# A sixteen-sequence RWKV, tree, attention and expert block: the products u times gate and the splitting of the maxima on GpSimd, and other figures in the planner

## The chip, the cores and the metric

The kernel runs on one core of a Trainium2 chip. The core has a matrix engine (TensorE, "PE" in the profile, its weight loads "PEld"), a vector engine (VectorE, "DVE"), a scalar engine with function tables (ScalarE, "ACT"), a general-purpose vector engine (GpSimd, "POOL"), and a queue that issues transfers ("SP"). Each works through its own queue of instructions in order, and waits on semaphores where it needs another's result. The metric is the device time of one execution in microseconds (us), the median of several executions.

## What is computed

The input x has 16 sequences of 512 tokens with 128 features. Four blocks follow each other, each with a residual and a layer norm:

```
x = layernorm(x + rwkv(x))       # two layer norms, time mix with a scan over the tokens, channel mix
x = layernorm(x + tree(x))       # 255 sigmoid routers, 256 leaf probabilities, leaf values
x = layernorm(x + attention(x))  # RMS norm, rotary positions, 16 heads of 8, causal softmax
x = layernorm(x + experts(x))    # 16 experts, the two of greatest gate kept, and a shared part
```

Two parts bear on the change. In the experts block, with u the normed input,

```
s = softmax(u @ centroids.T + bias)
g = s where s is one of the two greatest of its token, else 0
out = u + sum over e of g[e] * (u @ Wr[e].T + br[e]) + shared(u)
```

and in attention the softmax over the keys subtracts the greatest score of each query and head.

## The kernel before

Features (or the chunks of 128 of the 512 hidden ones) lie on the partitions, and the 512 tokens of one sequence run along a tile, so that most instructions work on 128x512 numbers in f32. A sequence passes through these pieces, each a Python generator:

- `front` (line 458): the first norms, RWKV, tree and the rotated queries and keys. RWKV runs in four chunks (`rwkv`, line 503), two of them at a time. Each has products k, r and v on TensorE, two scans over the tokens on VectorE (sk and skv), the sum sk on GpSimd, two more steps of skv and the reciprocal of sk on VectorE, and the product rw on GpSimd. TensorE then multiplies rw by the output weights into p.
- `operands` (697) loads queries and keys, split in three bf16 parts, for one of four groups of four heads, into one of three sets of buffers.
- `greatest` (718) makes all scores of a group on TensorE (sc), takes their maxima on VectorE (nmx, 128x16 numbers), splits these in three bf16 parts (nm3), transposes the parts on TensorE (pmx) and puts them as extra rows into the queries.
- `weighted`, `sums` and `ends` make the scores again, transposed (st), their exponentials on ScalarE (ew), the weighted sums on TensorE (o) and the attention's output up to u, the experts' input.
- `gating` (863) makes the gates. They go to DRAM and come back as gb, spread over the partitions, two experts to a transfer, in two buffers.
- `by_gate` (937) makes the experts' operands us = u * gate, one 128x512 product for each of 16 experts, in three buffers. `experts` (951) multiplies each by its weights and adds it into the bank acc; a buffer comes free with that product.

The order of the work isn't the order of the program text. A planner (`Plan`, line 55) holds all pieces in a queue by time, runs the one that is due first, and with each instruction moves that engine's clock on by a cost: `tensor_us` (154), `vector_us` (163), `pool_us` (172) and a cost for ScalarE. The instructions are issued in the order in which the planner comes to them, and `issue_after` (137) keeps that order on each engine. A bare `yield` hands over once the piece's last instruction is done by the planner's clock; slots stand for buffers and PSUM banks. The planner runs when the kernel is built. Its clock decides the order alone; on the chip only the order and the semaphores are left.

A front starts when the one before it has come to its event "mixed" (591, after its channel mix), but not before its due time by the planner's clock:

```python
yield event("mixed", b - 1)
yield max(0.0, PERIOD * b - LEAD - plan.now)
```

So several sequences are under way at once: RWKV of one, attention of the one before, and experts of the one before that.

Of the kernel before, what the change touches and what calls it, by code (L numbers as in the profile page):

```python
# [12 lines left out]
ALU = mybir.AluOpType  # L13
# [3 lines left out]
B, T, D = 16, 512, 128  # L17
# [23 lines left out]
HAND_OVER = 0.2  # L41
BANKS = 8
SCORES = 4
PERIOD = 125.0
LEAD = 60.0
RWKV_PACE = 10.0
EXPERT_PACE = 3.0
MAX_PACE = 0.0
# [98 lines left out]
def columns(ap):  # L147
    n = 1
    for d in ap.shape[1:]:
        n *= d  # L150
    return n


def tensor_us(op, out, w, x, *_):
    n = columns(out)
    if out.shape[0] == 32:
        return 0.05 + 0.0009 * n
    if x.dtype == BF16:
        return 0.02 + 0.00044 * n
    return 0.01 + 0.0009 * n if op == "transpose" else max(0.25, 0.00177 * n)  # L160


def vector_us(op, out, *args):
# [6 lines left out]


def pool_us(op, out, *_):
    return 0.5 + 0.0019 * columns(out)


@with_exitstack
def rwkv_tree_attn_moe(ctx: ExitStack, tc: tile.TileContext, a: dict, out: bass.AP):
# [18 lines left out]
    def scalar_us(op, out, x, f=None, *_):  # L196
        us, wanted = 0.2 + 0.00078 * columns(out), {AF.Ln: "ln", AF.Tanh: "tanh"}.get(f, table[0])
        if wanted != table[0]:
            table[0] = wanted
            us += 1.3  # L200
        return us

    mm, tr, act, copy = (Engine(plan, "PE", nc.tensor, tensor_us).matmul, Engine(plan, "PE", nc.tensor, tensor_us).transpose,
                         Engine(plan, "A", nc.scalar, scalar_us).activation, Engine(plan, "A", nc.scalar, scalar_us).copy)
    V, G = Engine(plan, "V", nc.vector, vector_us), Engine(plan, "G", nc.gpsimd, pool_us)
    banks, scores, chunks, sets = Slots(plan, BANKS), Slots(plan, SCORES), Slots(plan, 2), Slots(plan, OPERANDS)
    e_slots, us_slots, gb_slots = Slots(plan, 2), Slots(plan, 3), Slots(plan, 2)
    held, happened = {}, {}

    def event(*key):  # L210
        return happened.setdefault(key, Event(plan))
# [7 lines left out]
    def load_x(b):  # L219
        x0 = p2.tile([128, T], F32, tag="x0", name="x0")  # L220
        nc.sync.dma_start(out=x0, in_=a["xT"][:, b * T:(b + 1) * T])
        return x0
# [190 lines left out]
    def bank(name, shape=(128, 512), dtype=F32):  # L413
        i = yield banks
        p = ps.tile(list(shape), dtype, tag=f"b{i}", name=name)
        held[id(p)] = p, i
        return p

    def give(p):
        banks.put(held.pop(id(p))[1])  # L420
# [37 lines left out]
    def front(b, keep):  # L458

        if b:  # L460
            yield event("mixed", b - 1)
            yield max(0.0, PERIOD * b - LEAD - plan.now)
        x0 = load_x(b) if b else first_x
# [254 lines left out]
    def greatest():  # L718

        for b in range(B):  # L720
            for g in range(NG):
                yield event("ops", b, g)
                _, qo, ko = kept[b]["ops", g]
                nmx = p2.tile([128, NT, HG], F32, tag="nmx", name="nmx")
                for t in range(NT):
                    w = (t + 1) * 128
                    per = min(HG, 512 // w)
                    for h in range(0, HG, per):
                        slot = yield scores
                        sc = yield from bank("sc", (128, per, w))  # L730
                        for i in range(per):
                            mm(sc[:, i, :], qo[:, h + i, t * 128:w], ko[:, h + i, 0:w], start=(i == 0), stop=False)
                        mm(sc[:, :, t * 128:w], identb, masks[:, 0:per, :], start=False, stop=True)
                        yield
                        V.tensor_reduce(nmx[:, t, h:h + per], sc, AX.X, ALU.max, negate=True)
                        give(sc)
                        scores.put(slot)
                        if MAX_PACE:
                            yield MAX_PACE
                nm3 = p2.tile([128, NT, PARTS, HG], BF16, tag="nm3", name="nm3")  # L740
                V.tensor_copy(nm3[:, :, 0, :], nmx)
                V.tensor_tensor(nmx, nmx, nm3[:, :, 0, :], ALU.subtract)
                V.tensor_copy(nm3[:, :, 1, :], nmx)
                V.tensor_tensor(nm3[:, :, 2, :], nmx, nm3[:, :, 1, :], ALU.subtract)
                yield
                pt = yield from bank("pmx", (128, 512), BF16)
                for t in range(NT):
                    tr(pt[0:PARTS * HG, t * 128:(t + 1) * 128], nm3[:, t].rearrange("p a h -> p (a h)"), identb)
                yield
                rows = p2.tile([PARTS * HG, T], BF16, tag="rows", name="rows")  # L750
                copy(rows, pt[0:PARTS * HG, :])
                give(pt)
                for i in range(PARTS):
                    nc.sync.dma_start(out=qo[QK_ROWS + i:QK_ROWS + i + 1, :, :], in_=rows[HG * i:HG * (i + 1), :])
                plan.go(plan.end + 3.0, landed(b, g))

    def landed(b, g):
        event("max", b, g).set()
        return
        yield  # L760
# [176 lines left out]
    def by_gate():  # L937

        for b in range(B):
            for q in range(NE):  # L940
                yield event("gb", b, q // 2)
                slot = yield us_slots
                gb, slot_gb = kept["gb", b, q // 2]
                us = p3.tile([128, T], F32, tag="us", name="us")
                (G if q % 2 else V).tensor_tensor(us, kept[b]["u"], gb[:, q % 2, :], ALU.mult)
                if q % 2:
                    gb_slots.put(slot_gb)
                kept["us", b, q] = us, slot
                event("us", b, q).set()
# [35 lines left out]
    kept = {b: {} for b in range(B)}  # L985
    for b in range(B):
        plan.go(0.0, front(b, kept[b]))
    for piece in (prepare_mixes, prepare_tree, prepare_attention, prepare_experts, operands, greatest, weighted, sums, ends, gating, by_gate, experts):
        plan.go(0.0, piece())
# [54 lines left out]
```

## Time and profile before

| | |
|---|---|
| median of 3 runs | 2106.99 us (2105.85 to 2110.73) |
| profiled execution | 2105.58 us |
| its span, first to last instruction | 2103.8 us |
| PE busy | 1804.2 us (86%) |
| DVE busy | 1632.6 us (78%) |
| ACT busy | 1102.7 us (52%) |
| POOL busy | 640.3 us (30%) |
| us = u * gate on DVE | 128 instructions, 135.6 us |
| us = u * gate on POOL | 128 instructions, 199.2 us |
| splits of the maxima on DVE | 256 instructions, 49.9 us |

The profile is of one execution, and the durations of instructions are of that execution. "Busy" is the time in which an engine has an instruction under way. For TensorE the ends of instructions are modelled, so busy time there isn't the same as full speed. Almost all instructions are issued through the one line 138 of the recording helper, so a group is known by the tile that it writes. In a row with a bar, busy time and the mean in ns of one instruction follow the bar, then the engine's idle time just ahead of these instructions, and what ended it. In a row of the chain of waits stand the start in us, the length, the engine and the tile, with the number of instructions. In a row of windows stand the window, its length, and then the busy time and the instructions of PE, PEld, DVE, ACT and POOL, the granted TensorE clock, the DMA share and GB/s. In a row of one tile stand the shortest, median and longest instruction in ns.

### The profile page before, as it was taken

The numbers are of one execution on the slowest core, as the hardware profiler recorded it, in microseconds if no ns is written. First come the engines' busy times: TensorE is split into PE (matmuls) and PEld (weight loads), VectorE is DVE, ScalarE is ACT, GpSimd is POOL, SyncE is SP. The second block draws the span as 40 slices with busy tenths as digits, with TensorE's granted clock in tenths as the row PEclk, the third lists the DMA queues.
The fourth block names the chain that finished last, engine by engine and source line by source line (L and its number), as shares of the span: only waits on it lengthen the run. The fifth ranks groups of instructions, "written<-read, shape, count | busy, mean of one in ns | idle before, by whom it ended". The sixth has DMA issues, their size and how long they took to land.

```text
span 2103.8 us, 25637 instructions
## 1 busy us (share of the span) xinstructions
PE 1804.2 (86%) x8678; PEld 813.7 (39%) x8750; DVE 1632.6 (78%) x2631; ACT 1102.7 (52%) x1840; POOL 640.3 (30%) x588
## 2 busy tenths in 40 slices
PE   5557889888989989898998989899898989988895
PEld 1223344343434434343433434344343434434441
DVE  7586978779696987969698796969879696986442
ACT  2334656473645647274554727465472746545441
POOL 1141223224142341514234151523415151331222
PEclk9678999999999999999999999999999999999997
DMA  2001021112122121312212131222213121222322
GB/s 90 5 21 34 13 85 63 45 59 89 35 81 60 54 83 50 99 35 71 71 55 82 50 99 35 79 63 64 74 50 99 34 86 51 63 73 65 95 93 91
DMA packets 61971, 133.80 MB, mean 64 GB/s; under 512 B 11708, under 2 KB 32974, under 8 KB 61585
## 3 DMA queue, kind: packets, MB, share of 16 engines
q1 hardware_dynamic: 61841, 132.16, 20.2%
q8 instruction: 70, 1.15, 0.2%
q14 instruction: 60, 0.49, 0.1%
HBM read 114.01 MB, written 17.31 MB: 62 GB/s over the span
## 4 chain that ended last, share of the span: by engine, by line
DVE 44%; PE 36%; issue 5%; ACT 4%; POOL 3%; DMA 3%; SPq 0%; DVEq 0%; ACTq 0%; POOLq 0%
DVE sk L138 11%; DVE skv L138 8%; DVE nmx L138 8%; PE p L138 6%; DVE us L138 5%; PE sc L138 5%; PE o L138 4%; PE st L138 4%; PE acc L138 4%; PE pv L138 3%; PE ph L138 3%; DVE k L138 2%; DVE four L138 2%; DMA gb<-gd 1%; DVE kv L138 1%
## 5 line engine op out<-in xcount | busy, mean ns | idle before, releaser
L138 DVE TENSOR_REDUCE nmx<-sc 128x1 f32<-128x384 f32 (+3 forms) x704 | 432.3, 634 | 204.6 <-PE sc L138 192.2
L138 ACT ACTIVATE ew<-st 128x512 f32<-128x512 f32 (+1 forms) x704 | 381.1, 557 | 391.9 <-PE st L138 385.3
L138 PE MATMUL sc<-kop,qop 128*128 128x128 bf16 (+3 forms) x1012 | 256.0, 310 | 70.4 <-ACT t L138 63.9
L138 PE MATMUL acc<-us,w_mo 128*128 128x512 f32 x512 | 291.7, 654 | 15.5 <-DVE us L138 14.5
L138 PE MATMUL st<-qop,kop 128*128 128x512 bf16 (+1 forms) x1020 | 257.2, 306 | 26.3 <-ACT t L138 12.6
L138 POOL TENSOR_TENSOR us<-u,gb 128x512 f32<-128x512 f32 x128 | 199.2, 1556 | 210.2 <-PE acc L138 98.8
L138 PE MATMUL o<-ew,vaug 128*32 128x512 f32 (+3 forms) x2048 | 229.5, 468 | 13.5 <-ACT ew L138 4.5
L138 DVE RECIPROCAL sk<-sk 128x512 f32<-128x512 f32 x64 | 213.8, 3341 | 0.0
L138 POOL TENSOR_TENSOR dx<-xn 128x512 f32<-128x512 f32 x32 | 34.1, 1067 | 575.5 <-DVE xn L138 572.9
L138 DVE TENSOR_TENSOR us<-u,gb 128x512 f32<-128x512 f32 x128 | 135.6, 1066 | 54.4 <-DMA gb<-gd 35.5
L138 PEld LDWEIGHTS <-qop 128*128 128x128 bf16 x1024 | 97.2, 102 | 189.4 <-issue 158.9
L138 PE MATMUL sc<-masks,idents 128*128 128x128 bf16 (+2 forms) x683 | 169.2, 248 | 0.8 <-issue 0.3
L138 PEld LDWEIGHTS <-kop 128*128 128x128 bf16 x1024 | 87.8, 99 | 196.5 <-issue 164.0
L138 PE MATMUL st<-idents,masks 128*128 128x128 bf16 (+2 forms) x669 | 160.4, 240 | 0.2
L138 ACT ACTIVATE k<-k 128x512 f32<-128x512 f32 x64 | 40.0, 625 | 208.5 <-DVE k L138 208.5
L138 POOL TENSOR_TENSOR sk<-fk,sk 128x512 f32<-128x512 f32 x64 | 91.6, 1431 | 183.9 <-DVE sk L138 152.2
L138 PE MATMUL p<-rw,w_tm 128*128 128x512 f32 x128 | 78.7, 699 | 74.9 <-POOL rw L138 61.0
L138 POOL TENSOR_TENSOR rw<-skv,sk 128x512 f32<-128x512 f32 x64 | 88.4, 1382 | 173.2 <-DVE sk L138 173.2
L138 PEld LDWEIGHTS acc<-us,w_mo 128*128 128x128 f32 x512 | 92.8, 208 | 77.3 <-issue 37.5
L138 DVE SCALAR_TENSOR_TENSOR skv<-kv,first,skv 128x512 f32<-128x512 f32 x64 | 101.2, 1581 | 7.0 <-DVE skv L138 0.5
L138 DVE TENSOR_TENSOR_SCAN skv<-decay,kv 128x511 f32<-128x511 f32 x64 | 105.1, 1642 | 0.0
L138 PEld LDWEIGHTS <-idents 128*128 128x128 bf16 x704 | 70.8, 101 | 86.0 <-issue 80.6
(198 smaller groups left out, 3191.9 us busy)
## 6 DMA issues: line engine op xcount, KB each, us to landing
gb<-gd SPq DMA_DIRECT2D x128, 512.0 KB
qop<-there SPq DMA_DIRECT2D x576, 32.0 KB
kop<-there SPq DMA_DIRECT2D x192, 96.0 KB
there<-parts SPq DMA_DIRECT2D x32, 384.0 KB
x<-xT SPq DMA_DIRECT2D x16, 256.0 KB
out<-sqb SPq DMA_DIRECT2D x16, 256.0 KB
qop<-rows SPq DMA_DIRECT2D x192, 4.0 KB
w_mo<-w_mo SPq DMA_DIRECT2D x1, 1160.0 KB
```

Source lines behind the costliest of these rows:

```text
L138: ins = getattr(self.engine, op)(out, *args, **kw)
```

## The change

The products us all go to GpSimd (before, VectorE took the even experts), but for the odd experts of the last sequence, which VectorE takes. The four small instructions that split the maxima go to GpSimd, too, behind a hand-over (`yield`). In the planner the costs of TensorE are lowered (f32 products, those that write 32 rows, and the least cost of a small one), GpSimd's cost gets a smaller fixed part and a larger one per column, and the raster in which fronts are due goes from 125 to 115, with a lead of 40 for 60. The arithmetic stays as it is. Since the costs decide the order, the order of instructions changes on every engine.

```diff
-PERIOD = 125.0
-LEAD = 60.0
+PERIOD = 115.0
+LEAD = 40.0
...
 def tensor_us(op, out, w, x, *_):
     n = columns(out)
     if out.shape[0] == 32:
-        return 0.05 + 0.0009 * n
+        return 0.02 + 0.0007 * n
     if x.dtype == BF16:
         return 0.02 + 0.00044 * n
-    return 0.01 + 0.0009 * n if op == "transpose" else max(0.25, 0.00177 * n)
+    return 0.01 + 0.0009 * n if op == "transpose" else max(0.15, 0.00173 * n)
...
 def pool_us(op, out, *_):
-    return 0.5 + 0.0019 * columns(out)
+    return 0.25 + 0.0022 * columns(out)
...
                 nm3 = p2.tile([128, NT, PARTS, HG], BF16, tag="nm3", name="nm3")
-                V.tensor_copy(nm3[:, :, 0, :], nmx)
-                V.tensor_tensor(nmx, nmx, nm3[:, :, 0, :], ALU.subtract)
-                V.tensor_copy(nm3[:, :, 1, :], nmx)
-                V.tensor_tensor(nm3[:, :, 2, :], nmx, nm3[:, :, 1, :], ALU.subtract)
+                yield
+                G.tensor_copy(nm3[:, :, 0, :], nmx)
+                G.tensor_tensor(nmx, nmx, nm3[:, :, 0, :], ALU.subtract)
+                G.tensor_copy(nm3[:, :, 1, :], nmx)
+                G.tensor_tensor(nm3[:, :, 2, :], nmx, nm3[:, :, 1, :], ALU.subtract)
                 yield
...
                 us = p3.tile([128, T], F32, tag="us", name="us")
-                (G if q % 2 else V).tensor_tensor(us, kept[b]["u"], gb[:, q % 2, :], ALU.mult)
+                (V if b == B - 1 and q % 2 else G).tensor_tensor(us, kept[b]["u"], gb[:, q % 2, :], ALU.mult)
```

## The prediction

> **What bounds the kernel now.** I read the page's busy shares first, then the waits, then the chain of waits through one period, then the busy time cut at the places where that chain changes engine. The page alone misleads: TensorE is busy 86% and VectorE 78%, so neither looks full. The chain shows why. From about 720 us on it repeats every 122.6 us, one sequence each, and inside a period it lies on one engine for a long while and then on the other. Its two turning points, from the chain of waits of one period:
>
> ```profile
> 1061.43 0.77 DVE xn L138
> 1062.34 1.04 POOL dx L138
> 1063.40 0.75 DVE xk L138
> ...
> 1089.38 2.26 DVE us L138 x2
> ...
> 1132.66 3.27 DVE sk L138
> ...
> 1136.00 1.27 POOL rw L138
> ...
> 1137.32 1.13 PE p L138 x2
> ```
>
> From xn (the operand of the mixes) to the fourth reciprocal sk every step is VectorE's; after rw it is TensorE's until the next xn. Busy time cut there (length, then PE, PEld, DVE, ACT, POOL):
>
> ```profile
> 1061.40:1137.30 75.90, 65.44 (x304) 27.71 (x304) 73.59 (x94) 34.13 (x58) 36.72 (x33) 0.96 0.29 91
> 1137.30:1184.00 46.70, 45.65 (x254) 22.73 (x256) 28.85 (x67) 35.45 (x60) 3.98 (x5) 1.00 0.09 26
> ```
>
> The first stretch, D, is full on VectorE (73.6 of 75.9 us); the second, P, is full on TensorE (45.7 of 46.7). A period is D plus P. VectorE's time in D is thus worth its full price, and its time in P is worth nothing. The rows of the product u times gate within D say how much of it moves:
>
> ```profile
> L138 POOL TENSOR_TENSOR us<-u,gb 128x512 f32<-128x512 f32 x8 | 12.4, 1545 | 7.7 <-PE acc L138 5.2 <-DMA gb<-gd 2.5
> L138 DVE TENSOR_TENSOR us<-u,gb 128x512 f32<-128x512 f32 x8 | 8.4, 1054 | 0.0
> ```
>
> All 16 products of a sequence lie in D, eight on each engine.
>
> **What the Trainium skill says.** "Perfetto Trace Analysis", Optimization Strategy, says that a kernel can have several regimes with a different most-contended engine in each; D and P are that. "SBUF — State Buffer", Who interferes with whom, says that a VectorE instruction with two SBUF inputs contends with a GpSimd instruction that reads SBUF, the first to start holding the shared ports and the other blocking fully[...]. The trace agrees: the scan skv takes 1.19 us at its shortest and 1.66 in the median, skv from kv 0.75 and 1.51, the product us 0.62 and up to 1.77; the reciprocal stays between 3.32 and 3.35. "GPSIMD Engine Reference", Performance versus the Vector engine, has GpSimd about twice as slow at such a product (1.96 times); here the shortest are 1.26 us against 0.62.
>
> **The change, part by part.**
>
> *Order and raster.* The order of instructions of the changed kernel comes out the same with a raster of 1 as with 115: the due time never binds, each front simply starts at "mixed" of the one before. So PERIOD and LEAD mean only that the waiting to 125 is gone; what counts is the new order on each queue. In it the sequences keep their distance (the last front's queries begin at matmul 5962 instead of 5954 of 6535), so the drain after the last front keeps its length. The order repeats every three sequences instead of every one, which fits the three operand sets.
>
> *VectorE in D.* Counting the new order from xk to the fourth reciprocal, mean of six sequences: us 8 to 0, 8 x 1.054 = -8.4; the splits of the maxima 4 to 0, 4 x 0.2 = -0.8; max-reductions 18 to 19.7, 1.67 x 0.64 = +1.1; two small ones of the gating out, 2 x 0.22 = -0.4. Sum -8.5.
>
> *The shared ports.* In D the two-input instructions of the scans, skv and xv cost 10.4 us more than at their shortest: (1.44-1.20) x 4 + (1.81-1.19) x 4 + (1.80-0.75) x 4 + (1.13-0.69) x 4 + 1.05. GpSimd's work in D goes from 36.7 to 36.7 + 8 x 1.545 = 49.1 plus the splits. In proportion the blocking grows by a third, +3.5. Bounds: 0, if the products fall beside reciprocals and PSUM readers; 8, if every one of these instructions meets a GpSimd product. I take 3.5, and so D becomes 75.9 - 8.5 + 3.5 = 70.9.
>
> *TensorE.* It has 65.4 us of work in D, now of 70.9 (92%); by the order it gains 0.8 there and loses 0.8 in P (priced with the rows' busy time per product). P shows that it can run at 98%, but two nearly full queues in order stop each other; I add 1.0 (0 to 4). P becomes 46.7 - 0.8 = 45.9.
>
> *GpSimd.* In the part of D where its products lie (1084.3 to 1137.3) it is busy 29.9 of 53.0 us; with eight more products and about five splits at 0.25 it needs 43.6 of 48. That just fits. Queued behind each us, which waits for acc to free one of three buffers, are sk and rw, and for rw waits p on TensorE, now already 61 us over the run, plus 86 on its weight loads.
>
> *The splits on GpSimd.* No row has such a size on GpSimd; the copy 128x1 takes 0.18 to 0.65 us. Four in a chain: 0.7 to 2.6, I take 1.1 against 0.83 on VectorE (1092.88 to 1093.7), plus two hand-overs. Behind them in TensorE's order stand the transposes pmx; between the last scores of a group and pmx it has 5.0 us of other matmuls in the mean (4.4 before). Two of twelve groups have only 1.4 and 1.9; there I count 1 us each: 64/6 = 11 groups, of which half on the path, +5. Without any cover it would be 64 x 0.7 = 45.
>
> *Table loads on ScalarE* go from 132 to 156, 24 x 1.28 = 31 us. ScalarE is busy 35 of 47 us in P and 34 of 76 in D, and exponentials fill most of it; a load hurts only ahead of a normalisation. +5 (0 to 31).
>
> *The last sequence.* VectorE keeps eight of its products, now the odd ones. The drain there waits in turn for gb, and both engines still take one product of each pair: 0 (-4 to +4).
>
> **The sum.** Period 70.9 + 45.9 + 1.0 = 117.8, 4.8 less. Twelve sequences run in this pattern by the order (from the fifth on; before that the difference in the sum is small): -58. Earlier sequences -4, first gain at the fourth; splits +5, tables +5, drain 0: -52. Against the profiled execution's own 2105.6 us (span 2103.8 plus 1.8 around it) this gives 2053.6, and the median of the runs, 2107.0, lies 1.4 above that execution: 2055.
>
> **The rivals.**
>
> *Full relief:* the products land where VectorE reads PSUM or inverts, no blocking is added, and TensorE fills D too. Then D is 67.4, P 45.9, a period 113.3: 12 x -9.3 = -112, to 1995. For it: median us 0.69 on VectorE shows that half of them already met nobody. Against it: 43.6 of 48 us of GpSimd leaves little room for choice.
>
> *Nothing moves:* blocking and coupling near their upper ends (8 and 4) eat what VectorE and P give (8.5 and 0.8), and the period stays within a microsecond of 122.6: 2095 to 2120, 2107 in the middle. For it: both grow with GpSimd's load. Against it: both would have to be at their ends together.
>
> *GpSimd becomes the bound (slower):* its queue is strict, and a us that waits for acc holds rw behind it. Place: the last 53 us of D. Price: 43.6 of work, the waits for acc doubled with the products (5.2 to 10.4), the waits of rw for the reciprocal kept at 7.8: 61.8 against 53.0, +8.8 a period, 12 x 8.8 - 4 = +102, to 2209. It decides from the point where the waits that stay on GpSimd pass 9.4 us (53.0 - 43.6); below that, something of VectorE's gain is left. For it: the waits in that part add up to 26 us now. Against it: most of them are slack while VectorE is late, and the order puts three products ahead, one for each buffer.
>
> **How the numbers follow.** Forecast 0.53 (2020 to 2085), full relief 0.22, nothing moves 0.07, GpSimd's bound 0.18. About 0.2% is what a measurement of this kernel can tell from no change (4.2 us). Faster: 0.53 + 0.22 + 0.02 = 0.77; same 0.03; slower 0.18 + 0.02 = 0.20. The range leaves out most of the slower rival and the far end of the full relief: 1985 to 2110.
>
> **What would show it.** Right: the period in the chain near 118; VectorE's us down to 8 instructions; D still VectorE's but near 71, with skv and the scans longer in the mean (skv from kv above 1.58); GpSimd over 65% busy in D; TensorE's wait for rw no longer than now. Wrong: a chain with GpSimd's us in D and TensorE waiting for us or rw (the slower rival); scans no longer than before and a period under 115 (full relief); TensorE waiting for nm at every group (the splits mispriced).

## The result, and the profile after

The changed kernel takes 2083.8 us in the median of four runs (2081.6 to 2086.8), the kernel before 2106.4 beside it: a ratio of 0.9889, with a 95% interval of 0.9871 to 0.9908. That is 23 us less, not the 52 that the prediction summed. Where do they come from? The mark "xn of the front" divides the spans: the first five sequences take 12.2 us less, the ten periods after them 7.1, and what follows the last front's start 5.0. The sum had 58 for twelve periods in the repeating pattern, so that pattern is where the forecast went wrong.

Page of the changed kernel, the chain that ended last, shares of the span by engine:

```profile
PE 39%; DVE 28%; ACT 11%; POOL 7%; DMA 5%; issue 4%; SPq 1%; POOLq 0%; DVEq 0%; ACTq 0%
```

Before it was VectorE 44%, TensorE 36%, ScalarE 4%. VectorE's share fell as meant, but the rest of the chain now changes engine more often. The busy time of the changed kernel, cut as before at xn and at the fourth reciprocal, for three sequences in a row, D and P in turn (length, then PE, PEld, DVE, ACT, POOL, each with its instructions):

```profile
1043.26:1119.08 75.82, 65.75 (x316) 29.22 (x308) 66.43 (x83) 37.46 (x60) 46.60 (x47) 0.93 0.26 86
1119.08:1168.30 49.22, 46.22 (x257) 22.74 (x260) 26.24 (x55) 38.22 (x62) 7.18 (x15) 1.00 0.12 33
1168.30:1239.04 70.74, 60.27 (x291) 25.44 (x290) 64.90 (x83) 32.91 (x55) 49.53 (x46) 1.00 0.28 91
1239.04:1288.57 49.53, 45.44 (x229) 21.87 (x228) 24.95 (x55) 36.90 (x60) 6.15 (x12) 0.94 0.10 31
1288.57:1361.11 72.54, 65.49 (x306) 29.14 (x310) 65.80 (x83) 33.30 (x56) 50.73 (x45) 0.93 0.28 93
1361.11:1407.97 46.86, 44.30 (x253) 21.71 (x253) 25.46 (x55) 34.88 (x59) 7.50 (x17) 1.00 0.10 30
```

In the prediction's row of before, VectorE was busy 73.6 of D's 75.9 us. (That row runs to the end of rw, 1.4 us past the reciprocal; cut at the reciprocal, the mean of six is 72.6 of 74.9.) Now VectorE is busy some 66 and D is still 71 to 76 long. VectorE isn't full in D any more, and no other engine is either. What VectorE waits for in D (us in all, times, longest): in the D of before that the prediction shows (1061.40 to 1137.30), then in the first and the second D of the rows above:

```profile
DVE xn L138 <- ACT r L138: 1.2, 1, 1.2
DVE xk L138 <- POOL dx L138: 0.6, 1, 0.6
```

```profile
DVE nmx L138 <- PE sc L138: 4.0, 2, 3.7
DVE four L138 <- PE pa L138: 1.8, 2, 1.1
DVE xn L138 <- ACT r L138: 1.7, 1, 1.7
DVE xk L138 <- ACT xx L138: 1.7, 1, 1.7
DVE kv L138 <- PE pvv L138: 0.4, 1, 0.4
```

```profile
DVE k L138 <- PE pk L138: 1.8, 1, 1.8
DVE four L138 <- PE pb L138: 1.5, 1, 1.5
DVE kv L138 <- PE pvv L138: 1.1, 1, 1.1
```

The wait before xn lies ahead of D. In six D's of the changed kernel TensorE is named for 33 of 36 us of such waits. But TensorE isn't full in D (60 to 66 us of 71 to 76). Its own waits, in D and P together, first in seven periods of the kernel before (814 to 1672 us), then in seven of the changed one (800 to 1650 us):

```profile
PE sc L138 <- ACT t L138: 44.2, 14, 4.0
PE p L138 <- POOL rw L138: 18.8, 7, 2.8
PE pout L138 <- DVE rb L138: 3.5, 7, 0.5
```

```profile
PE pmx L138 <- POOL nm L138: 15.3, 7, 3.2
PE p L138 <- POOL rw L138: 12.1, 11, 2.5
PE pg L138 <- ACT t L138: 11.2, 4, 3.3
PE o L138 <- ACT t L138: 9.9, 3, 3.3
PE sc L138 <- DVE nmx L138: 8.4, 9, 1.3
PE acc L138 <- POOL us L138: 5.2, 6, 2.1
```

Before, two places made most of TensorE's waiting, and VectorE hardly waited in D. Now each queue stops at many places for another one. The products themselves are cheap where they are now: 248 of them on GpSimd, and little blocking added to the scans on VectorE (median 1.66 us before, now 1.64). From the groups of instructions, that of us on GpSimd (busy time, mean ns of one, then GpSimd's idle time ahead of it and what ended it):

```profile
L138 POOL TENSOR_TENSOR us<-u,gb 128x512 f32<-128x512 f32 x248 | 366.5, 1493 | 120.9 <-DMA gb<-gd 85.1 <-PE acc L138 35.1
```

And from the tile skv, the three instructions of the scan on VectorE (shortest, median and longest in ns):

```profile
L138 DVE TENSOR_TENSOR_SCAN skv<-decay,kv x64: 1191/1636/2931, 30.0 to 1840.8; 128x511 f32<-128x511 f32 x64
L138 DVE SCALAR_TENSOR_TENSOR skv<-kv,first,skv x64: 750/1505/2371, 32.4 to 1842.6; 128x512 f32<-128x512 f32 x64
L138 DVE SCALAR_TENSOR_TENSOR skv<-t,skv x64: 691/1561/2420, 33.2 to 1844.2; 128x512 f32<-128x512 f32 x64
```

Only the last, skv times t, has gone from 0.69 to 1.56 us in the median. The one before it, skv from kv, which was to rise above 1.58 us in the mean, has fallen to 1.37.

### The profile page after: what moved, and what is told of

It is laid out like the page before. It is cut to its first block, busy times and chain, and to the rows that moved or that the text cites. A ratio compares the mean times of both kernels' runs of the same rounds, so it can differ in the third digit from the quotient of the medians.

```text
span 2079.5 us, 25567 instructions
## 1 busy us (share of the span) xinstructions
PE 1777.2 (85%) x8750; PEld 809.4 (39%) x8750; DVE 1483.0 (71%) x2255; ACT 1141.8 (55%) x1864; POOL 870.2 (42%) x964
## 4 chain that ended last, share of the span: by engine, by line
PE 39%; DVE 28%; ACT 11%; POOL 7%; DMA 5%; issue 4%; SPq 1%; POOLq 0%; DVEq 0%; ACTq 0%
PE p L138 7%; DVE sk L138 7%; DVE nmx L138 6%; DVE skv L138 6%; PE acc L138 5%; PE st L138 4%; PE o L138 4%; PE sc L138 4%; POOL us L138 3%; DMA gb<-gd 3%; PE ph L138 3%; PE pv L138 3%; ACT ew L138 2%; ACT L435 2%; ACT r L138 2%
## 5 line engine op out<-in xcount | busy, mean ns | idle before, releaser
L138 POOL TENSOR_TENSOR us<-u,gb 128x512 f32<-128x512 f32 x248 | 366.5, 1493 | 120.9 <-DMA gb<-gd 85.1
L138 PE MATMUL acc<-us,w_mo 128*128 128x512 f32 x512 | 279.7, 635 | 18.0 <-POOL us L138 18.0
L138 PE MATMUL st<-qop,kop 128*128 128x512 bf16 (+3 forms) x1024 | 257.5, 306 | 20.4 <-DMA qop<-rows 10.0
L138 POOL CAST nm<-nmx 128x16 bf16<-128x16 f32 x128 | 37.0, 289 | 450.2 <-DVE nmx L138 446.0
L138 PE MATMUL o<-ew,vaug 128*32 128x512 f32 (+3 forms) x2048 | 210.5, 453 | 15.4 <-ACT t L138 12.4
L138 PE MATMUL st<-idents,masks 128*128 128x128 bf16 (+2 forms) x704 | 173.8, 247 | 0.0
L138 POOL TENSOR_TENSOR sk<-fk,sk 128x512 f32<-128x512 f32 x64 | 99.5, 1555 | 78.0 <-PE sc L138 44.7
L138 PEld LDWEIGHTS acc<-us,w_mo 128*128 128x128 f32 x512 | 85.7, 196 | 80.3 <-issue 36.2
L138 DVE TENSOR_TENSOR_SCAN sk<-decay,k 128x511 f32<-128x511 f32 x64 | 104.5, 1632 | 0.0
L138 PE MATMUL pv<-sq,mean_w 128*128 128x512 f32 x160 | 91.0, 652 | 13.7 <-ACT sq L138 13.6
```

The lines of the kernel that those rows point to most:

```text
L138: ins = getattr(self.engine, op)(out, *args, **kw)
```

## The experiments

All ratios are to the kernel before, run on the same chip beside it. D, P and VectorE's busy and idle time in D are means in us over six sequences, the eighth to the thirteenth, cut at the same marks in each profile:

| run | ratio (95%) | D | VectorE busy | idle | P |
|---|---|---|---|---|---|
| before | 1 | 74.9 | 72.6 | 2.3 | 47.4 |
| changed | 0.9889 (0.9871 to 0.9908) | 73.1 | 65.7 | 7.4 | 48.4 |
| after_noload | 0.9845 (0.9828 to 0.9861) | 71.4 | 65.1 | 6.3 | 48.8 |
| before_noload | 0.9951 (0.9936 to 0.9965) | 75.0 | 72.8 | 2.2 | 46.1 |
| after_nmV | 1.0182 (1.0167 to 1.0197) | 74.9 | 69.7 | 5.2 | 50.7 |
| engines_only | 0.9873 (0.9855 to 0.9891) | 75.1 | 66.6 | 8.5 | 45.7 |
| plan_only | 1.0144 (1.0129 to 1.0159) | 76.9 | 70.8 | 6.1 | 48.0 |
| order_before_engines_after | 1.0138 (1.0123 to 1.0154) | 75.5 | 62.9 | 12.6 | 48.6 |
| order_after_engines_before | 1.0437 (1.0420 to 1.0455) | 79.6 | 72.3 | 7.3 | 51.3 |
| order_after_nmV | 1.0220 (1.0200 to 1.0239) | 75.5 | 67.6 | 7.9 | 51.0 |
| after_us_copy | 0.9628 (0.9605 to 0.9651) | 69.6 | 62.0 | 7.6 | 48.0 |
| after_pool_memset | 1.0624 (1.0604 to 1.0644) | 80.3 | 64.6 | 15.6 | 52.9 |
| after_us12 | 1.0288 (1.0248 to 1.0328) | 79.8 | 69.6 | 10.2 | 49.1 |
| after_fit | 0.9900 (0.9879 to 0.9920) | 71.7 | 61.3 | 10.4 | 47.4 |
| after_nomask | 0.9776 (0.9760 to 0.9793) | 72.7 | 65.5 | 7.2 | 47.9 |
| before_nomask | 0.9948 (0.9933 to 0.9963) | 74.8 | 72.6 | 2.2 | 46.8 |
| after_all_three | 0.9466 (0.9439 to 0.9494) | 68.9 | 61.9 | 7.0 | 47.0 |

### Table loads

Both kernels without the table loads, with a planner that still counts them, so that the order of the other instructions stays (but for a few transfers on SP):

```diff
-        if table[0] == "ln":
-            act(r, var, AF.Ln, bias=bias, scale=scale)
-        else:
-            with tc.issue_after(plan.last["A"].ins):
-                tab = nc.scalar.preload_act_table_set("natural_log_exp_and_others")
-            plan.last["A"] = tab
-            act(r, var, AF.Ln, bias=bias, scale=scale)
+        if table[0] != "ln":
+            table[0] = "ln"
+            plan.did("A", 1.3)
+        act(r, var, AF.Exp, bias=bias, scale=scale)
```

> The changed kernel without any table load after the first: the logarithm of each normalisation is taken as an exponential (so the normalised values aren't the reference's), the order of instructions stays. Theory 1 (the 24 added table loads, four of them in a row in the stretch P, are why the period fell by 1.4 us and not by 4.8): at least 45 us faster than the changed kernel, and a gain at least 20 us greater than that of the same edit on the kernel before. Rival (the order without slack, or GpSimd): the gain is the same on both within 8 us.

> The kernel before with the same edit, order kept (normalised values aren't the reference's). Theory 1: 10 to 25 us faster than before, as D is VectorE's and P TensorE's there. Rival: as much as on the changed kernel, 25 to 45 us on both.

It took 0.44% off the changed kernel (0.9889 to 0.9845), some 9 us, and 0.49% off the one before, some 10. The gains are alike, as the rival had it, but smaller than it said. So the first theory falls: the 24 added loads are not where the forecast gain went. P doesn't shrink on the changed kernel at all.

### The splits, and the planner's figures

`after_nmV` puts the four splitting instructions back on VectorE (G to V in the five lines of the diff) and plans anew. `engines_only` has the new placement, but the costs, raster and lead of before.

> The changed kernel with the splits of the maxima back on VectorE, all else as changed, the order planned anew. Theory 2 (GpSimd's splits come late: TensorE and its weight loads wait 81 us for nm, against 28 before): 15 to 30 us faster than the changed kernel. Theory 1 and theory 3 (order): 5 to 12 us slower, 0.8 us of VectorE for each group in D.

> The products and splits on GpSimd as changed, but the planner's costs, raster and lead of before (125 and 60). Theory 3 (the new costs and the missing raster leave an order without slack, in which VectorE and TensorE stop each other): 2050 to 2065, faster than the changed kernel. If the new costs and raster bring part of the gain: 2085 to 2105.

Both expectations missed. With the splits on VectorE the kernel is 2.9% slower than the changed one (1.0182 against 0.9889), more than the 50 us that they took there before. A reason shows in the tile of the splits:

```profile
L138 DVE CAST nm<-nmx x128: 174/174/2043, 178.2 to 2067.9; 128x16 bf16<-128x16 f32 x128
L138 DVE TENSOR_TENSOR nmx<-nmx,nm x64: 174/175/2042, 179.4 to 2067.7; 128x16 f32<-128x16 f32 x64
L138 DVE TENSOR_TENSOR nm<-nmx,nm x64: 174/175/1241, 179.8 to 2068.1; 128x16 bf16<-128x16 f32 x64
```

An instruction of 0.17 us now takes up to 2.04. 50 of the 256 take over 0.4 us. Each of these starts while a GpSimd instruction is under way, in half of the cases a product us, and ends 0.03 to 0.10 us after that one. They take 91 us in all for 50 before. And `engines_only` is as fast as the changed kernel (0.9873, the intervals overlap). So the gain comes with the new placement, planned anew, and the new costs and the raster bring nothing beside it. The planner then ran with the new costs and the old placement:

> The planner's new costs, raster and lead with the products and splits where they were before (even experts and splits on VectorE), planned anew. If the planner's figures bring part of the gain by themselves: 0.990 to 0.998. If they bring none, as the run with the old figures and the new placement says (0.9873 against 0.9889): 1.000 to 1.020, because the tighter order meets VectorE's full load in D.

The figures alone make it 1.4% slower, as the second reading expected.

### Order and placement apart

A planner that reckons with one engine while the instruction goes to another's queue keeps the order of all others. Every instruction then has the place in the order that it would have had, only in the other queue:

```diff
-    def __init__(self, plan, name, engine, cost):
+    def __init__(self, plan, name, engine, cost, queue=None):
+        self.queue = queue or name
...
+    VG = Engine(plan, "V", nc.gpsimd, vector_us, "G")
+    GV = Engine(plan, "G", nc.vector, pool_us, "V")
...
-                (G if q % 2 else V).tensor_tensor(us, kept[b]["u"], gb[:, q % 2, :], ALU.mult)
+                (G if q % 2 else V if b == B - 1 else VG).tensor_tensor(us, kept[b]["u"], gb[:, q % 2, :], ALU.mult)
```

> The planner and so the order of before; only the products us of the even experts (but for the last sequence's) and the splits go to GpSimd's queue instead of VectorE's, each at the same place in the order. Theory 3 (relief of VectorE in D by 8.5 us, less what the shared ports and the coupling of the queues take back): ratio to before 0.980 to 0.990. If placement gives what the prediction summed (4.8 us a period): 0.975 or less. If the gain came from the new order: 0.997 or more.

> The order of the changed kernel, but the even experts' products and all splits are in VectorE's queue again, at their places in that order. If the order alone brought the gain: ratio to before 0.985 to 0.995. If placement brought it: 1.000 to 1.015, as VectorE has its 8.5 us in D again.

> The order of the changed kernel, only the splits in VectorE's queue again at their places. If the kernel with the splits on VectorE was 61 us slower because of its newly planned order: at most 20 us slower than the changed kernel (ratio to before 0.985 to 0.998). If the splits themselves cost that on VectorE: ratio 1.010 to 1.020. If GpSimd's splits come late and that matters: faster than the changed kernel, below 0.985.

Together they answer the main question, though against both readings. The first run fits "gain from the new order", the second then contradicts it: it was to be 0.985 to 0.995, or at the most 1.015, and is 1.0437. The third lies just above its expected span. So the change is made of two parts which are each a loss without the other: the new placement in the old order +1.4%, the new order with the old placement +4.4%. Together they are -1.1%.

In the old order the new placement does for VectorE all that was summed, and more: its work in D falls from 72.6 to 62.9. But its idle time grows from 2.3 to 12.6. The waits of that run name GpSimd, first over the whole run, then TensorE's and VectorE's longest in one D (951.08 to 1025.56 us):

```profile
PEld p L139 <- POOL rw L139: 196.9, 44, 10.7
PE p L139 <- POOL rw L139: 173.7, 42, 9.9
```

```profile
PE p L139 <- POOL rw L139: 8.9, 2, 4.9
DVE nmx L139 <- PE sc L139: 5.7, 3, 2.8
DVE four L139 <- PE pa L139: 2.6, 1, 2.6
```

Before, TensorE waited 61 us for rw in the whole run, and its weight loads 86. This is the slower rival of the prediction: rw stands behind products us or splits in GpSimd's queue, p waits for rw in TensorE's, and the scores for VectorE's maxima come behind p. The newly planned order avoids most of it: the changed kernel waits 67 and 83 us there. Which of its shifts does that isn't shown: p stands later in it at some chunks and earlier at others.

In the new order VectorE's idle time in D hardly depends on the placement: 7.3 with the products and splits on VectorE, 7.9 with the splits alone, 7.4 as changed. There D shrinks from 79.6 to 73.1, by 6.5, which is VectorE's work (72.3 to 65.7). So the placement pays its price in full where the order stays the same; the new order costs some 5 us of VectorE's idle time in D, against the old one with the old placement, and 3.9 us in P. A third order with the old placement, that of `plan_only`, leaves VectorE 6.1 us idle in D. So the order by itself moves the idle time, from 2.3 to 6.1 and 7.3. The splits alone, back on VectorE, lengthen P by 2.6 us, as much as D (2.4), so what VectorE does in P isn't free in this order.

### Is one engine the bound of D now?

Four runs, order kept, change the load of GpSimd or of TensorE. `after_us_copy` makes us a copy of the gate, without the factor u, `after_pool_memset` adds eight small writes of zeros behind each product, and the two "nomask" kernels leave out the mask under the maxima:

```diff
-                (V if b == B - 1 and q % 2 else G).tensor_tensor(us, kept[b]["u"], gb[:, q % 2, :], ALU.mult)
+                (V if b == B - 1 and q % 2 else G).tensor_copy(us, gb[:, q % 2, :])
```

```diff
+                for _ in range(8 if b < B - 1 else 0):
+                    with tc.issue_after(plan.last["G"].ins):
+                        plan.last["G"] = nc.gpsimd.memset(spare, 0.0)
```

```diff
-                            mm(sc[:, i, :], qo[:, h + i, t * 128:w], ko[:, h + i, 0:w], start=(i == 0), stop=False)
-                        mm(sc[:, :, t * 128:w], identb, masks[:, 0:per, :], start=False, stop=True)
+                            mm(sc[:, i, :], qo[:, h + i, t * 128:w], ko[:, h + i, 0:w], start=(i == 0), stop=(i == per - 1))
+                        plan.did("PE", tensor_us("matmul", sc[:, :, t * 128:w], identb, masks[:, 0:per, :]))
```

> The changed kernel, order kept, but the operand us is a copy of the gate, without the factor u (so the experts' part is another): one SBUF input for two, and so a shorter GpSimd instruction. If blocking at the shared ports and GpSimd's lateness keep the gain small: at least 25 us faster than the changed kernel (ratio 0.977 or less). If the coupling of TensorE's and VectorE's queues does: within 10 us of it (0.984 to 0.990).

> The changed kernel, order kept, with eight writes of 128x1 zeros into a spare tile on GpSimd behind each product us of the first fifteen sequences (0.1 us each by the row of such a write, so at most 13 us a period, at least 4; they read nothing, so VectorE isn't blocked). If GpSimd's lateness is what VectorE waits for in D: 35 us or more above the changed kernel (ratio to before 1.005 or more). If the blocking at the shared ports and the order of the other queues keep the gain small: within 12 us of it (0.983 to 0.995).

> The changed kernel, order kept, without the product that adds the causal mask to the scores of which only the maxima are taken (maxima over the later keys of the diagonal block too): TensorE has about 10 us less a period. If VectorE's 7.4 us of idle time in D is TensorE's lateness: D falls by 4 us or more besides P, in all 70 us or more below the changed kernel (ratio to before 0.956 or less). If other engines make that idle time: D falls by less than 2, the whole by 30 to 55 us (0.963 to 0.975).

> The kernel before with the same product left out, order kept. As D is VectorE's there, only P falls, by up to 5 us: 35 to 60 us below before (0.971 to 0.983), and D by less than 1.5. If TensorE's lateness is in D there too: D falls by 3 or more, 0.965 or less.

The copy took 55 us off (0.9889 to 0.9628). GpSimd had 10.8 us less to do in D, and VectorE was less blocked: its work fell from 65.7 to 62.0, and D by 3.5, nearly the same. The idle time stayed (7.6). So at the shared ports the sixteen products cost VectorE 3.7 us a period more than copies do. What they cost in all is more by what the copies block, which no run shows. Beyond that, less work of GpSimd's own gives D nothing.

More work does lengthen D: the added writes made the kernel 155 us slower, and GpSimd has the largest share of the chain that ended last in that run:

```profile
POOL 31%; PE 28%; DVE 15%; ACT 9%; issue 7%; DMA 5%; SPq 0%; POOLq 0%; DVEq 0%; ACTq 0%
```

This overstates GpSimd's part, as TensorE's weight loads then wait 48 us in all, and its products 24, for these writes, which they don't need. But it agrees with what the prediction said of GpSimd's work: it just fits.

Both runs leave a rival in part open: the clock that TensorE is granted, as a share of its full speed. It was 0.939 in the mean of the runs before, 0.944 for the changed kernel, 0.956 for the copy and 0.924 for the added writes. A run's span times what the clock lacks to 1 is an estimate of the time that this can cost at most: 128, 117, 90 and 170 us. So up to 27 of the copy's 55 us and up to 53 of the 155 us could be the clock's. For the change itself the clock is slightly better than before, so it is not what ate the forecast gain.

Without the mask product the changed kernel is 1.1% faster (24 us), and D falls by 0.4 us only; the kernel before gains 0.5% (11 us). Both fall short of what was expected, since the edit relieves TensorE by less: the products left out have durations of 175 us in all, but TensorE's busy time falls by 52 (1777.2 to 1725.1), and in D by 1.9 (63.3 to 61.4). So this speaks against TensorE's load as what VectorE waits for in D, but the relief is too small to refute it. All three edits together:

> The changed kernel, order kept, with all three edits: no table loads, us as a copy of the gate, no mask product under the maxima (normalised values and experts aren't the reference's). Alone they took 9, 55 and 23 us off and left VectorE 6.3, 7.6 and 7.2 us idle in D. If several nearly full engines together make that idle time: more than the sum, at least 100 us below the changed kernel (ratio to before 0.941 or less), and the idle time in D under 5 us. If it is the order itself, each hand-over in turn: the sum or less (0.947 or more), and the idle time stays at 6 to 8 us.

The gains add up: 0.44 + 2.61 + 1.13 = 4.18% alone, 4.23% together. VectorE's idle time in D is 7.0. ScalarE is relieved by 5.1 us in D there, GpSimd by 10.6 and TensorE by 2.9, and the idle time is nearly what it was. With the runs of other orders this makes the order itself the likely cause, the places where one queue stops for another. A greater relief of TensorE alone is untested, and which of these hand-overs carry the idle time, the runs don't say.

### Other orders

`after_us12` gives every fourth product to VectorE, `after_fit` takes VectorE's and GpSimd's costs from the changed kernel's profile:

```diff
-                (V if b == B - 1 and q % 2 else G).tensor_tensor(us, kept[b]["u"], gb[:, q % 2, :], ALU.mult)
+                (V if (q % 2 if b == B - 1 else q % 4 == 0) else G).tensor_tensor(us, kept[b]["u"], gb[:, q % 2, :], ALU.mult)
```

```diff
-        return 0.3 + 0.0023 * n
-    return 0.2 + 0.00108 * n
+        return 0.3 + 0.0026 * n
+    if op == "scalar_tensor_tensor":
+        return 0.1 + 0.0018 * n
+    return 0.13 + 0.00107 * n
...
-    return 0.25 + 0.0022 * columns(out)
+    return 0.2 + 0.0026 * columns(out)
```

> As changed, but every fourth product of the first fifteen sequences on VectorE (12 of 16 on GpSimd), planned anew. If GpSimd is overloaded in D with 16: faster than the changed kernel, 0.975 to 0.985. If VectorE's time in D decides: 4 x 1.05 us more a period, half of it on the path, 12 x 2 = 25 us slower, 0.998 to 1.005.

> As changed, but with costs of VectorE and GpSimd taken from the profile of the changed kernel (GpSimd's product 1.5 us, scans 1.6, the three-operand instructions 1.0, others 0.68), so that the order expects the blocking that happens. If a better fitting order gives the missing gain: 0.965 to 0.980. If the order can't help, because the ports decide: 0.984 to 0.995.

With twelve products on GpSimd the kernel is 4% slower than with sixteen, far beyond the price of four products on VectorE: another order again, with 10.2 us idle in D. How much is the order's and how much the placement's isn't separated here. The fitted costs gave an order in which VectorE has less to do in D (61.3) and is idle longer (10.4), and no gain over the changed kernel. Last, the mask product left out of the planner's sums too, with the new figures, with the old ones (raster 125), and with the fitted costs:

> The same product left out of the changed kernel and of the planner's sums, so that the order is planned for it. If order and durations must fit: 10 us or more faster than with the order kept. If the order doesn't matter: within 10 us of it.

> As the last, with the planner's costs, raster and lead of before. If the new costs and raster matter no more than in the first comparison (0.9873 against 0.9889): within 15 us of the last run. If the raster of 125 binds: 20 us or more slower.

> A try for a better version: the mask product under the maxima left out, and the costs of VectorE and GpSimd from the changed kernel's profile. If the better costs help the order once TensorE has room: 0.965 to 0.975, below the 0.9776 of the version without the mask product alone. Otherwise 0.975 to 0.985.

They came to 0.9769 (0.9747 to 0.9790), 0.9849 (0.9834 to 0.9864) and 0.9882 (0.9851 to 0.9912). The first is as fast as with the order kept. The second is 16 us slower than the first, between its two expectations, and the third is slower than both of its own: in these two orders leaving out the mask product brings no gain that is clear. The mask isn't needed under the maxima: the softmax doesn't depend on the number subtracted, as long as nothing over- or underflows, and the scores of the second product keep their mask. So `after_nomask`, at 2059.0 us, and its newly planned twin at 2058.7 are the best versions found, 2.2 to 2.3% below the kernel before.

## Why the prediction missed

**What bounds the kernel: right for D, in part for P.** The runs of the order before show D on VectorE too: without mask or table loads D stays within 0.2 us and only P shrinks. But P shrinks more without ScalarE's table loads (1.3 us) than without TensorE's mask product (0.6), so TensorE alone isn't all of P.

**VectorE in D (-8.5), the shared ports (+3.5): near.** Together -5.0; its busy time fell by 6.9. If the -8.5 is right, the ports cost 1.6 more than before, not 3.5. What the Trainium skill says of a VectorE instruction with two SBUF inputs beside one of GpSimd that reads SBUF ("SBUF — State Buffer", Who interferes with whom) agrees with the changed kernel: the scan skv takes 1.19 to 2.93 us there, while the reciprocal, with one input, stays between 3.32 and 3.35. But one input alone is no safeguard: of the 50 splits held up in `after_nmV`, 28 are casts.

**TensorE ("two nearly full queues in order stop each other; I add 1.0"): this step failed.** VectorE's idle time in D went from 2.3 to 7.4, +5.1 for +1.0, where the bounds were 0 to 4. I had asked what each engine has to do in D in the new order, and taken over the 2.3 us of idle time from the old one. In the new order the idle time hardly follows the load: in seven profiles of the new order, the changed kernel's and those with other loads on VectorE, TensorE, ScalarE or a lighter GpSimd, it is 6.3 to 7.9. With a heavier GpSimd it is 15.6.

**P ("becomes 46.7 - 0.8"): wrong in sign.** It went from 47.4 to 48.4 by the mean of six. Half of that is TensorE's own work (45.1, then 45.6), which was to fall; the rest is idle time. Not the table loads: without them P is 48.8. With the old figures of the planner, and the new placement, P is 45.7, but D 75.1. So how the two stretches share the time depends on the order, too. The period came out at 121.6 for 122.3, a fall of 0.7 and not of 4.8. Three terms make that difference of 4.1, but for rounding: 4.1 us more idle time, 1.8 more in P, and 1.9 less work of VectorE.

**Order and raster ("what counts is the new order on each queue"): half right.** I counted the instructions in each stretch of that order and found little moved, and so gave the order no price. It had one, of both signs: with the old placement it costs 4.4%, with the new one it is worth 2.5% (1.0138 against 0.9889).

**GpSimd ("just fits"): right.** With less of its work D falls by no more than VectorE's own work does (3.5 and 3.7); with the added writes D grows by 7.2. In the old order the slower rival came true in kind, with TensorE waiting for rw at its place, though it cost 28 us and not 102.

**Splits (+5), tables (+5), drain (0).** TensorE waits 33 us for the splits, and its weight loads 48, but on VectorE they would cost 70 us more in the same order. All table loads together cost 9 us in the changed kernel and 10 in the one before, so the 24 added ones cost nothing that shows; their +5 lies within the noise of this comparison. The start and the end came out 17 us better than in the kernel before, where the sum had 4 for earlier sequences and nothing for the end. That the time still lies within the forecast's 2020 to 2085 is luck: most of the gain comes from the start and the end, and not from the pattern that was summed.

## What to carry to other kernels

Moving work from a full engine in a kernel of fixed queues has a price that no count of busy time shows: the order decides how long each queue stops for the others, and a move that pays in one order can lose in another. So keep the order and move only the queue in one run, and keep the placement and change only the order in another, before a gain is put down to either. And when an engine's work falls but its stretch doesn't shrink as much, look at its idle time in that stretch: if freeing the others one by one and then all together leaves it, and another order moves it, look for the cause in the order. Check first in the busy time how much an edit really frees: the mask product's durations promised three times what leaving it out gave.

## What the runs showed of the hardware

Small VectorE instructions lose most in proportion at the shared ports. In `after_nmV` a split of 128x16 numbers takes 0.17 us at its shortest and up to 2.04 behind a GpSimd instruction; the cast, with its one SBUF input, is held up like the others. On GpSimd itself the same four, in the changed kernel, take 0.19 to 0.22 us each at their shortest, so that for so small a tile GpSimd is hardly slower than VectorE, while its product of 128x512 takes twice as long (1.26 against 0.62 us at the shortest).

A wait of TensorE can cost more than its length. In the profiles before and after, TensorE's granted clock drops from 1 to 0.5, for some 3.4 us or a multiple of it, 56 times after the first 500 us. Each drop begins within 3 us of the end of a TensorE wait of over 1 us, and of the 29 waits of over 3 us, 28 have a drop beside them. In the changed kernel the products acc that lie wholly in such a drop take 1.06 to 1.22 us, those outside 0.59 to 0.70. One drop of the changed kernel, behind a wait of 3.2 us for the splits: the stretch before it and the drop itself (the clock is the third number from the end):

```profile
869.71:873.12 3.41, 0.72 (x2) 0.00 (x0) 3.30 (x4) 0.00 (x0) 3.27 (x5) 1.00 0.17 59
873.12:879.95 6.83, 5.84 (x14) 2.57 (x15) 2.87 (x4) 1.66 (x3) 1.77 (x4) 0.50 0.15 48
```
